# AdaLN block on one core: the feed-forward weight sums in two buffers, one sum emitted with each projection

## The chip, the cores and the metric

The kernel runs on one core of a Trainium2 chip. The metric is the device time of one execution in microseconds; the kernel before took 1318.79 us in the median of three runs (1311.11, 1318.79 and 1322.47). Engines are named as the profile names them: PE is TensorE (matmuls and transposes), DVE is VectorE, ACT is ScalarE, POOL is GpSimd, and SP is the sync engine, which here only issues DMAs. "SPq", "POOLq" and "ACTq" are the DMA-issuing instructions on those engines. Each engine runs its own instructions strictly in the order in which they were built, so an instruction that waits holds up all that stand behind it on its engine.

## The reference

The reference is one transformer block with adaptive layer norm, for 4 batches of 512 tokens of width 512, in float32:

```
mod = (silu(c) @ wmod)  ->  sa, ca, ga, sb, cb, gb          # per batch, width 512
h = layernorm(x) * (1 + ca) + sa
x = x + ga * attention(h)          # gated delta rule, 6 heads, key 64, value 128
h = layernorm(x) * (1 + cb) + sb
x = x + gb * ffn(h)                # (silu(h @ w_gate.T) * (h @ w_up.T)) @ w_down.T, hidden 2048
```

The attention projects h to q, k and v (each followed by a causal convolution of four taps and silu), to a gate, and to two small scalars per head and token (a decay and a beta). A recurrent state per head is decayed, corrected by the delta rule and read out token by token; the read-out is normalised, multiplied by silu(gate) and projected back to width 512. ga and gb are pushed away from zero to a size of at least 0.25.

## The kernel before, in words

Tokens are handled per batch b (0 to 3); a batch has four tiles of 128 tokens, and a tile two chunks of 64. The program has these parts:

- `first_normed_t`, `normed_t`: layer norm of a batch's x, and its transpose `ht` (features by tokens). `load_x(b)` brings the batch's x in, four chunks of 128 x 512. For batches 0 and 2 the four chunks are slices of one tile; for batches 1 and 3 they are four tiles of the tag `xt`, which has four buffers.
- `keys`, `queries`, `values`, `gates`: projections. One `weight` load (L249, on SP's queue, tag `w`, four buffers) serves one head or pair of heads, for the batches in its list. A projection is four matmuls (L478). Keys, queries and values go through `conv_silu` (ACT L486, three DVE operations L488, ACT L492). `by_token` turns a value projection to tokens (PE L559, DVE L561, tag `v`, two buffers) and stores it in DRAM from SP's queue (L565).
- `between(i)` is called after each projection of `values` and `gates`. It runs, on odd i, one step of the modulation for later batches.
- `triangles(b)`: the 32 x 32 triangular inverses of a batch. A chain of small DVE operations (L656, L660) ends in the tiles `ti` and `pm`, which SP stores to the DRAM tensors `td` and `ttd` (L664, L665); SP then loads them back in pieces (L709 to L711) as operands `t` and `lm`.
- `delta_rule(b)`: for each of four tiles, `operands` (PE L689 to L732), `scan` (PE L753, L762) and `finish` / `project` / `turned`. `finish` squares the output on POOL (L784, tile `osq`), and scales it on POOL (L790, tile `o`) once DVE has the norm; `project` transposes it (PE `pot` L799), multiplies by Wo (PE L803) and adds the residual on POOL (L806, tile `xr`); `turned` transposes the normed result `xn` (DVE L814, PE `pxn` L820). The PE work of other projections is interleaved with it.
- `weight_sums`: the feed-forward uses a seven-product scheme for 2 x 2 blocks of the gate and up weights, which needs four sums of weight blocks for each pair of hidden tiles. For each of 8 pairs and for the gate and the up weights (16 sums in all) it loads four blocks (four DMAs of 128 x 2 x 128 on SP's queue, L861), makes four additions on POOL (L866 to L869, each 128 x 256) and stores the 128 x 7 x 2 x 128 result to the DRAM tensor `wsum` from POOL's queue (L870). The tile is of the tag `wm`, which has one buffer, so the loads of one sum wait until the store of the sum before has landed. The tiles are called `wsg` (gate) and `wsu` (up) below.
- `feed_forward(b)` reads `wsum` back (L920, L921) and does the products (PE L927, L899).

The order of the work is the order of emission, reshaped by a scheduler: it places each engine's instructions by a priority (the place in the program) and by when it reckons that their inputs are ready. An instruction emitted early can so stand late on its engine, and an independent one emitted later can stand ahead of it. The emission around the change is: values, triangles and gates of batch 0, `delta_rule(0)`, keys and queries of batches 1 to 3, all of `weight_sums()`, then values and gates of batch 1, `triangles(1)`, values of batches 2 and 3, `delta_rule(1)`, gates of 2 and 3. On the engines, `delta_rule(0)` runs beside those keys, queries and sums.

Of the kernel before, what the change touches and what calls it, by code (L numbers as in the profile page):

```python
# [8 lines left out]
F32 = mybir.dt.float32  # L9
# [6 lines left out]
P = 128  # L16
B, T, D = 4, 512, 512
H, DK, DV = 6, 64, 128
FF = 2048
NT = T // P  # L20
# [17 lines left out]
def adaln_block(  # L38
# [29 lines left out]
    w1 = ctx.enter_context(tc.tile_pool(name="w1", bufs=1))  # L68
# [4 lines left out]
    pa_ = stage_a.enter_context(tc.tile_pool(name="pa", bufs=2))  # L73
# [77 lines left out]

    def load_x(b):

        if b in (0, 2):
            room = w1.tile([P, NT, D], F32, tag="hf", bufs=2, name=f"xt{b}")
        if b == 0:
            for c in (0, 2):
                sp.dma_start(
                    room[:, c : c + 2], x[b, c * P : (c + 2) * P, :].rearrange("(c p) f -> p c f", p=P)
                )  # L160
            return [room[:, c, :] for c in range(NT)]
        ts = []
        for c in range(NT):
            t = room[:, c, :] if b == 2 else pa_.tile([P, D], F32, tag="xt", bufs=4, name=f"xt{b}_{c}")
            if b < 3:
                after(t[:1, :1])
            (act if b > 2 else pool).dma_start(t, x[b, c * P : (c + 1) * P, :])
            ts.append(t)
        return ts
# [11 lines left out]
    early_load(act, 0)  # L181
    sp.dma_start(c_in, c_t.rearrange("(k p) b -> p k b", p=P))
    xts = load_x(0)
    early_load(sp, KD // 2)

# [1 line left out]
    act.activation(warm, eps, AF.Silu)  # L187
    act.activation(sc_t[:, :, :B], c_in, AF.Silu)

    last, steps = [], []  # L190

    def between(i):

        if i % 2 and steps:
            steps.pop(0)()


    def after(t):

        pool.tensor_copy(t, last[0][:1, :1])  # L200
# [68 lines left out]
    for i in range(2):  # L269
# [14 lines left out]
        t = stat.tile([P, H, C], F32, name=f"xs{i}")  # L284
# [224 lines left out]
    def keys(bs, hts):  # L509
        if bs == [0]:  # L510
            betas, store = decays(bs, hts)
        sk = {}
        for i, b in enumerate(bs):
            sk[b] = pa_.tile([P, H, NT], F32, tag=f"sk{i}", bufs=1, name=f"sk{b}")
        for p in range(NP):
            w = first_w if bs == [0] and p == 0 else weight(w_k, p, f"k{bs[0]}_{p}")
            for b in bs:
                n = f"k{b}_{p}"
                kt = conv_silu(w, cw["k"], p, hts[b], n)
                act.dma_start(kd[b][:, p, :], kt)  # L520
                lagging(lambda a=(kt, sk[b], p, 1.0, n): squares(*a), 3 if bs == [0] else 2)
            if p == 1 and bs != [0]:
                betas, store = decays(bs, hts)
            if p < 2 and bs == [0]:
                xts[p + 1] = load_x(p + 1)
            if p == (1 if bs == [0] else 2):
                store()
        def scalars():
            for i, b in enumerate(bs):
                act.activation(nk[b], sk[b], AF.Sqrt)  # L530
                pool.tensor_scalar(nk[b], nk[b], -1.0, None, ALU.mult)
                vec.reciprocal(sc[b], sk[b])
                vec.scalar_tensor_tensor(sc[b], sc[b], -1.0, betas[:, i], ALU.mult, ALU.mult)

        lagging(scalars)
# [12 lines left out]
    def values(bs, hts):  # L548
        for h in range(H):
            w = weight(w_v, h, f"v{bs[0]}_{h}")  # L550
            for b in bs:
                vt = conv_silu(w, cw["v"], h, hts[b], f"v{b}_{h}")
                lagging(lambda a=(b, h, vt): by_token(*a))
                between(h)
# [12 lines left out]
    def gates(bs, hts):  # L567
        for h in range(H):
            w = weight(w_g, h, f"g{bs[0]}_{h}")
            for b in bs:  # L570
                pg = projected(w, hts[b], f"g{b}_{h}")
                sg = pa_.tile([P, T], F32, tag="acc", bufs=4, name=f"sg{b}_{h}")
                act.activation(sg, pg, AF.Silu)
                act.dma_start(
                    sd[b][:, :, h, :].rearrange("c v i -> v c i"), sg.rearrange("p (c i) -> p c i", c=NT)
                )
                if tails:
                    tails.pop(0)()
                between(h)


    ex, at, td, ttd, hf = {}, {}, {}, {}, {}
# [255 lines left out]
    def complete():  # L838
        while pending:
            pending.pop(0)()  # L840
# [11 lines left out]
    def weight_sums():  # L852

        for i in range(NF // 2):
            for src, dst, nm in ((w_gate_t, wsum[0], "g"), (w_up_t, wsum[1], "u")):
                w = pa_.tile([P, 7, 2, P], F32, tag="wm", bufs=1, name=f"ws{nm}{i}")

                for a, rows in enumerate((w[:, 0:2], w[:, 4:7:2])):
                    cols = slice((2 * i + a) * P, (2 * i + a + 1) * P)
                    for h in range(2):  # L860
                        sp.dma_start(  # L861
                            rows[:, h],
                            src[h * TH : (h + 1) * TH, cols].rearrange("(k p) f -> p k f", p=P),
                        )
                a11, a12, s2, s1, a21, s4, a22 = (w[:, j] for j in range(7))
                pool.tensor_add(s1, a21, a22)  # L866
                pool.tensor_sub(s2, s1, a11)
                pool.tensor_sub(a21, a11, a21)
                pool.tensor_sub(s4, a12, s2)  # L869
                pool.dma_start(dst[i], w)  # L870
# [113 lines left out]
    for b in rest[2:]:  # L984
        hts[b] = normed_t(b, load_x(b))
# [4 lines left out]
    keys(rest, hts)  # L990
    queries(rest, hts)
    complete()
    weight_sums()
    values([1], hts)
    gates([1], hts)
    triangles(1)
# [65 lines left out]
```

## Time and profile before

| quantity | value |
|---|---|
| median of 3 runs (range) | 1318.79 us (1311.11 to 1322.47) |
| the profiled execution's own time | 1315.23 us |
| its span | 1313.5 us |
| PE busy | 1242.2 us, 95% |
| DVE busy | 713.9 us, 54% |
| ACT busy | 386.3 us, 29% |
| POOL busy | 249.3 us, 19% |
| mean granted PE clock | 0.98 |

Durations below come from the one profiled execution. Its time is 1.7 us more than its span, and 3.6 us less than the median. Idle time of an engine matters only where that engine holds up the end; PE is busy for 95% of the span, so about 71 us of it are left as PE idle time, plus what PE loses where its granted clock is below 1.

### The profile page before, as it was taken

Reading aid. Unit: us, or ns where it says so; the run is one execution under the profiler, and the core shown is the slowest. Engines: PE = TensorE matmul, PEld = TensorE weight load, DVE = VectorE, ACT = ScalarE, POOL = GpSimd, SP = SyncE. Lnnn points to the kernel's source line nnn. Section 1 sums busy time; section 2 is a strip of 40 time slices with the busy share of each in tenths; the row PEclk is TensorE's granted clock in tenths of the full one; section 3 lists DMA queues with packets and bytes.
Section 4 is the critical chain, followed back from the end, with each engine's and each line's share of the span. In section 5 each row is a group of like instructions: output and inputs, shape, how many; then the busy total and the mean of one; then the engine's idle time right before and its main releaser. Section 6 shows DMA issues by size and latency. Waiting matters only on the chain.

```text
span 1313.5 us, 18027 instructions
## 1 busy us (share of the span) xinstructions
PE 1242.2 (95%) x6620; PEld 777.2 (59%) x6620; DVE 713.9 (54%) x1547; ACT 386.3 (29%) x740; POOL 249.3 (19%) x299
## 2 busy tenths in 40 slices
PE   6899898899999998989999999899999999999998
PEld 3444355444444565757757666676666577576665
DVE  4767765555288245774445558644464444444443
ACT  3643346643142344211103332110234211011110
POOL 4210223543200012020021121011111201111111
PEclk9889999999999999999999999899999999999999
DMA  5979647767955447664335455443622243354331
GB/s 154 267 186 285 200 119 227 186 213 225 276 165 161 118 108 184 204 178 134 126 115 163 124 124 164 134 144 101 185 78 71 94 144 116 117 189 143 117 112 64
DMA packets 213271, 204.06 MB, mean 155 GB/s; under 512 B 95032, under 2 KB 163640, under 8 KB 213184
## 3 DMA queue, kind: packets, MB, share of 16 engines
q1 hardware_dynamic: 191408, 167.14, 44.6%
q0 software_dynamic: 4096, 20.99, 4.2%
q10 hardware_dynamic: 17680, 14.78, 3.5%
q8 instruction: 53, 0.87, 0.3%
q14 instruction: 34, 0.28, 0.1%
HBM read 152.94 MB, written 46.78 MB: 152 GB/s over the span
## 4 chain that ended last, share of the span: by engine, by line
PE 66%; DVE 13%; DMA 9%; POOL 4%; issue 3%; ACT 2%; SPq 1%; POOLq 0%; ACTq 0%; DVEq 0%
PE phg L927 15%; PE pd L899 15%; PE phu L927 11%; PE pwo L803 5%; PE pp_v L478 3%; PE pp_g L478 2%; PE pm L762 2%; DVE ti L660 2%; DVE tip L656 2%; PE scratch L689 2%; DMA wsum<-wsu 1%; PE pf L753 1%; DMA wsum<-wsg 1%; PE pp_k L478 1%; DMA wsg<-in_w_gate_t_dram 1%
## 5 line engine op out<-in xcount | busy, mean ns | idle before, releaser
L899 PE MATMUL pd<-wdn,hid 128*128 128x512 f32 x512 | 225.5, 593 | 0.0
L905 POOL TENSOR_TENSOR xm<-xm,tmpf 128x512 f32<-128x512 f32 x64 | 81.3, 1270 | 451.9 <-DVE tmpf L904 451.9
L899 PEld LDWEIGHTS pd<-wdn,hid 128*128 128x128 f32 x512 | 97.7, 191 | 109.2 <-issue 102.6
L927 PE MATMUL phg<-hf,wg 128*128 128x256 f32 x512 | 138.6, 388 | 0.3 <-DMA wg<-wsum 0.3
L927 PEld LDWEIGHTS phg<-hf,wg 128*128 128x128 f32 x512 | 96.4, 193 | 21.4 <-issue 7.3
L927 PE MATMUL phg<-hs,wg 128*128 128x256 f32 x384 | 103.4, 389 | 4.4 <-DVE hid L934 4.3
L927 PE MATMUL phu<-hf,wu 128*128 128x256 f32 x384 | 99.9, 384 | 2.1 <-DMA wu<-wsum 2.0
L904 DVE TENSOR_TENSOR tmpf<-pd,gb 128x512 f32<-128x512 f32 x64 | 44.1, 689 | 104.0 <-PE pd L899 93.0
L927 PE MATMUL phu<-hs,wu 128*128 128x256 f32 x384 | 96.1, 384 | 3.5 <-DVE up L940 3.5
L478 PE MATMUL pp_v<-ht,wv 128*128 128x512 f32 x192 | 93.6, 632 | 4.5 <-DVE v L561 2.3
L932 ACT COPY hid<-phg 128x256 f32<-128x256 f32 x32 | 11.9, 371 | 288.8 <-PE phg L927 286.5
L803 PE MATMUL pwo<-wo,ot 128*128 128x512 f32 x192 | 93.3, 617 | 0.0
L478 PE MATMUL pp_g<-ht,wg 128*128 128x512 f32 x192 | 91.4, 618 | 1.6 <-issue 1.6
L927 PEld LDWEIGHTS phu<-hs,wu 128*128 128x128 f32 x384 | 72.4, 191 | 22.0 <-DVE up L940 9.0
L927 PEld LDWEIGHTS phg<-hs,wg 128*128 128x128 f32 x384 | 71.6, 194 | 18.3 <-DVE hid L934 5.8
L927 PEld LDWEIGHTS phu<-hf,wu 128*128 128x128 f32 x384 | 71.3, 191 | 15.0 <-issue 5.2
L478 PEld LDWEIGHTS pp_v<-ht,wv 128*128 128x128 f32 x192 | 36.9, 202 | 46.2 <-issue 43.4
L488 DVE SCALAR_TENSOR_TENSOR acc_v<-pp_v,conv_v,acc_v 128x511 f32<-128x511 f32 (+2 forms) x72 | 53.3, 743 | 8.8 <-ACT acc_v L486 8.1
L478 PEld LDWEIGHTS pp_g<-ht,wg 128*128 128x128 f32 x192 | 35.1, 195 | 38.2 <-issue 37.0
L956 ACT ACTIVATE hid<-hid 128x1024 f32<-128x1024 f32 x32 | 33.8, 1057 | 79.9 <-DVE hid L940 63.5
L762 PE MATMUL pm<-r,l 128*128 128x128 f32 x384 | 52.7, 283 | 1.0 <-ACT r L758 0.8
L803 PEld LDWEIGHTS pwo<-wo,ot 128*128 128x128 f32 x192 | 34.4, 192 | 30.1 <-issue 28.3
(236 smaller groups left out, 1812.8 us busy)
## 6 DMA issues: line engine op xcount, KB each, us to landing
wdn<-in_w_down_t_dram SPq DMA_DIRECT2D x32, 512.0 KB, 4.3
wg<-wsum SPq DMA_DIRECT2D x32, 512.0 KB, 3.7
wu<-wsum SPq DMA_DIRECT2D x32, 512.0 KB, 3.6
wg<-wsum SPq DMA_DIRECT2D x32, 384.0 KB, 4.3
wu<-wsum SPq DMA_DIRECT2D x32, 384.0 KB, 4.4
wsum<-wsg POOLq DMA_DIRECT2D x8, 896.0 KB, 4.0
wsum<-wsu POOLq DMA_DIRECT2D x8, 896.0 KB, 4.5
wg<-in_w_g_dram SPq DMA_DIRECT2D x24, 256.0 KB, 3.2
```

The lines of the kernel that those rows point to most:

```text
L478: pe.matmul(pp, w[:, k, :], ht[:, k, :], start=(k == 0), stop=(k == KD - 1))
L488: vec.scalar_tensor_tensor(acc[:, i:], pp[:, : T - i], taps[:, col, TAPS - 1 - i : TAPS - i], acc[:, i:], ALU.mult, ALU.add,)
L656: vec.tensor_tensor(v, pm[:, j, j + 1 :, None].broadcast_to([n, m, j]), t[:, j : j + 1, :j].broadcast_to([n, m, j]), ALU.mult,)
L660: vec.tensor_add(t[:, j + 1 :, :j], t[:, j + 1 :, :j], v)
L689: pe.matmul(pv[:, u, 2 * par : 2 * par + 2, :], kc[i][us, p, par : par + 2, :], qc[i][us, p, par : par + 2, :], start=True, stop=True,)
L762: pe.matmul(pm[:, h], l[:, hs.start + h, 2 * par : 2 * par + 2, :], r[:, par, hs.start + h], start=True, stop=True,)
L803: pe.matmul(pw, ot[:, h, :], wo[:, h, :], start=(h == 0), stop=(h == H - 1))
L899: pe.matmul(pd, hids[q, i // 2][:, i % 2, c * P : (c + 1) * P], wdn[q, i // 2][:, i % 2, :], start=(i == 0), stop=(i == NQ - 1),)
L904: vec.tensor_mul(tmp, pd, gb)
L905: pool.tensor_add(xm[c], xm[c], tmp)
L927: pe.matmul(o, l[:, k], r[:, k], start=k == 0, stop=k == 1)
L956: act.activation(hid, hid, AF.Silu)
```

## The change

All 16 sums stay, with the same loads, additions and stores. Three things move:

- `weight_sums` becomes a generator that stops ahead of each sum. `between` advances it by one step after each projection of `values` and `gates`. The first step only reaches the first stop, so the 16 sums are emitted after the 2nd to the 17th of those projections: five with the values of batch 1, six with its gates, five with the values of batches 2 and 3.
- The gate sums keep the buffer of tag `wm`; the up sums take the buffer of tag `xt`. Both tiles are declared as 128 x 4 x 512 and the first 14 x 128 columns are used.
- The x of batches 1 and 3 is one tile of tag `xt` with one buffer, instead of four tiles with four buffers. The bytes are the same.

```diff
     def load_x(b):
-        if b in (0, 2):
-            room = w1.tile([P, NT, D], F32, tag="hf", bufs=2, name=f"xt{b}")
+        room = (w1 if b in (0, 2) else pa_).tile(
+            [P, NT, D], F32, tag="xt" if b % 2 else "hf", bufs=1 if b % 2 else 2, name=f"xt{b}"
+        )
...
         for c in range(NT):
-            t = room[:, c, :] if b == 2 else pa_.tile([P, D], F32, tag="xt", bufs=4, name=f"xt{b}_{c}")
+            t = room[:, c, :]
...
-    last, steps = [], []
+    last, steps, sums = [], [], []
     def between(i):
         if i % 2 and steps:
             steps.pop(0)()
+        if sums and next(sums[0], 1):
+            sums.clear()
...
         for i in range(NF // 2):
             for src, dst, nm in ((w_gate_t, wsum[0], "g"), (w_up_t, wsum[1], "u")):
-                w = pa_.tile([P, 7, 2, P], F32, tag="wm", bufs=1, name=f"ws{nm}{i}")
+                yield
+                room = pa_.tile([P, NT, D], F32, tag="wm" if nm == "g" else "xt", bufs=1, name=f"ws{nm}{i}")
+                w = room.rearrange("p c f -> p (c f)")[:, : 14 * P].rearrange(
+                    "p (j k f) -> p j k f", j=7, k=2
+                )
...
     complete()
-    weight_sums()
+    sums.append(weight_sums())
     values([1], hts)
```

## The prediction

> **What bounds the kernel now.** I read the page's busy shares first: PE is busy for 95% of the span, so a change pays only where it closes a PE gap or lifts PE's granted clock. Then the chain that ended last, cut to the stretch in which the sums run (120 to 365 us):
>
> ```profile
> 311.75 2.67 DMA wsg<-in_w_gate_t_dram
> 314.59 0.71 POOL wsg L866
> ...
> 317.78 3.88 DMA wsum<-wsg
> 322.13 0.46 SPq L861
> ...
> 346.86 0.51 SPq L861
> 347.46 3.84 DMA wv<-in_w_v_dram
> 351.44 1.10 PE pp_v L478 x2
> ```
>
> From 257 us on this chain holds no PE work at all: load, four additions, store, next load, sixteen times one after the other in one buffer, until a value weight (wv) that stood behind the last sum on SP's queue comes in and PE goes on. What SP waits for, in the waits of its queue (us in all, times, longest):
>
> ```profile
> SPq L861 <- DMA wsum<-wsg: 31.7, 7, 7.2
> SPq L861 <- DMA wsum<-wsu: 30.0, 5, 7.6
> ```
>
> So SP stands 61.7 us in front of a sum's load, waiting for the store ahead to land, and whatever is behind on the queue is late by that. What this costs PE, in the waits of PE from 150 to 160, 210 to 260 and 320 to 356 us:
>
> ```profile
> PE scratch L717 <- DMA t<-td: 3.5, 1, 3.5
> ...
> PE pxn L820 <- DVE xn L814: 3.3, 2, 2.3
> PE pot L799 <- POOL o L790: 1.9, 1, 1.9
> PE pot L799 <- POOL gyt L460: 1.5, 1, 1.5
> ...
> PE pvt L559 <- DVE v L561: 3.1, 1, 3.1
> PE pp_v L478 <- DMA wv<-in_w_v_dram: 1.8, 1, 1.8
> PE pp_g L478 <- issue: 1.6, 1, 1.6
> ```
>
> A gap costs more than its length. In the table by stretch (length; busy and count of PE, PEld, DVE, ACT, POOL; clock; DMA share; GB/s) the clock is 1.00 before the gap at 154 to 158 us, and then:
>
> ```profile
> 155.00:160.00 5.00, 2.16 (x20) 0.93 (x20) 1.21 (x3) 0.51 (x1) 0.00 (x0) 0.85 0.59 163
> 160.00:165.00 5.00, 5.00 (x33) 1.91 (x32) 1.12 (x2) 1.77 (x4) 0.00 (x0) 0.50 0.25 39
> 165.00:170.00 5.00, 5.00 (x51) 1.89 (x50) 0.36 (x1) 0.62 (x2) 0.00 (x0) 0.96 0.22 66
> ```
>
> That is 5 x (0.15 + 0.50 + 0.04) = 3.45 us of PE's work lost. The same sum gives 1.6 us after the gaps at 215 to 225 (clock 0.68 in 225 to 230) and 0.4 + 1.3 = 1.7 us around the gap at 327 (0.92, then 0.74).
>
> The Trainium skill ("TensorE: Matmul & The Clock Gate", "What's actually happening") says that PE's clock halves after an idle window of about 3.4 us. The drop after 225 us follows gaps of 1.1, 1.2 and 1.5 us only; by the rule, a middle stage like it would not drop, and the sum below would end 1.6 us less far down at its best end.
>
> **The change, part by part.** Nothing is added on any engine: 64 loads, 64 additions (0.73 us) and 16 stores before and after. Only waits and places change. I compared the order in which the two kernels, as built, stand on each engine.
>
> *A. td behind a sum (154 to 166 us).* DVE ends the chain of batch 0's triangles at 147.3 us (last L660), but SP issues the store td only at 152.22, because the first load of the third sum stands ahead of it and waits for the second sum's store until 151.8. In the changed order the first up sum has its own buffer: its loads stand at about 129 to 135 us instead of 139.3 to 141.4, its additions follow the gate's (131.5 to 134.7), so they run at about 137.5 to 140.4, and with 4.3 us of store it lands near 145. The load that stands ahead of td waits for this store. td so goes out when DVE is done, at 147.5 to 149: 3.2 to 4.7 us earlier, against a PE wait of 3.5. With the gap, the half clock behind it goes. Ends: nothing (if the additional 2.8 MB of a second pair of sums, some 11 us at the 250 GB/s of this stretch, push the store's landing back to 151) and 3.5 + 3.45 = 6.9 us. I take 6, near the upper end, since td has 3 us to spare over what is needed.
>
> *B. The end of delta_rule(0) (215 to 256 us).* PE is busy for 32.7 of these 41 us; with the clock the stage can give 8.3 + 1.6 = 9.9 us, and the other end is a loss: POOL now has 11 sums instead of 6 ahead of the second tile's scaling, on which PE's pot waits:
>
> ```profile
> 222.23 0.73 POOL L869 TENSOR_TENSOR wsu<-wsu 128x256 f32<-128x256 f32 x1
> 223.26 0.60 POOL L870 DMA_DIRECT2D wsum<-wsu  x1 [0.30 <-POOL wsu L869]
> 223.88 1.48 POOL L790 TENSOR_TENSOR o<-o,ms 128x768 f32<-128x768 f32 x1
> ```
>
> DVE's part of it is ready at 220.9, so POOL's sum costs 3 us here. I followed the new queue on from A: the fifth gate sum and the first half of the fifth up sum stand ahead of the first xr; they are loaded at about 195.5 and 200 and added until 205.4, 2 us late for a scan that is 6 us ahead. xn, xr of the second tile and the last of the sixth gate sum's loads follow it (about 213), the additions run until 219, and the scaling starts at 219, 4.9 us earlier than now. So about 1 to 2 us of A are given back here. Then the order helps: xr of the second tile (now 237.35, held 2.2 us by a sum; tmpa was ready at 235.2) and the scaling of the third tile have no late sum ahead, and the DVE scans of batch 1 (1.2 and 3.93 us, now between 239 and 246) stand earlier: the waits of 2.3 and 1.9 us go. Together +2 us, nearer to nothing than to 9.9, because the first half shifts waits rather than ends them.
>
> *C. The gates and values after it (323 to 353 us).* Three stalls are SP's lateness: v (its buffer is freed by a store that stood behind a sum), a gate weight (shown as "issue"; its load went out at 325.4) and wv. In the new order all 64 loads stand ahead of the second value weight of batch 1, so none is left in front of these. 3.1 + 1.6 + 1.8 + 1.7 of clock = 8.2 us at most; nothing at the other end, if the sums come out as late as now. I take 7. PE was busy without a gap from 256 to 323 us, so it is PE itself that comes earlier. What is late next is DVE in 353 to 430 us (18 of each 20 us); it starts earlier by as much, since it idles from 323 to 353 (4.8 us busy in 30).
>
> *D. Crowding.* 16 instead of 12 sums stand ahead of the last xmid store of delta_rule(0): four more times four issues of 0.47 us, and 5.6 MB, some 25 us at 225 GB/s in a stage whose DMA share is 0.56 to 0.69. Hidden behind PE's filled 166 to 215 and 256 to 323 us; if not, each issue is late by up to 2 us per sum. I take -1; ends 0 and -8 (four sums by 2 us).
>
> The Trainium skill ("SBUF — State Buffer", "Who interferes with whom") speaks against crowding: a DVE operation in a two-port mode is blocked for the whole of a GpSimd instruction. Here xn took 1.67 us beside osq at 215.2 and 0.55 otherwise; by the rule a sum's addition beside each of four xn would make D up to 2.9 us worse.
>
> *E. x as one tile.* The instructions and the waits of each chunk are the same in both orders; nothing, either way up to 0.5 us for one issue.
>
> Sum: 6 + 2 + 7 - 1 = 14 us, from the profiled execution's 1315.2: **1301 us**. The median of the runs shown is 3.6 us above that execution, so 1301 is 1.3% below the median; runs of this kernel lie 11 us apart, and about 1% (13 us) is what a measurement can tell from no change.
>
> **The rivals.**
>
> 1. *The middle gives A back.* If the second tile's scaling on POOL comes no earlier than 224 us, A's 6 are gone at 224 and only C stays: 1315 - 7 = 1308. For it: 11 sums are ahead of it and each needs a landing; against it, the 4.9 us worked out above.
> 2. *The change doesn't act.* The sums still come one after the other, since SP issues in order and each load waits for scan operands ahead of it: stalls move but stay, 0 to 3 us, 1313. Against: the buffer that a load waits for was freed one sum earlier.
> 3. *Slower: the scan of batch 0 becomes bound by the sums.* Place: POOL, the scaling of the second tile behind the 11th sum. The first sum is added at 131.5; the 11th holds the scaling up beyond today's 223.9 once a sum takes more than (223.9 - 131.5) / 10 = 9.2 us. Where nothing else stood ahead, one buffer took 12.0 us a sum (first additions at 290.2 to 349.9, five intervals), so two buffers should take 6 to 7. If the two do not overlap and it stays at 11, the scaling comes at about 245: 21 us late, 1.7 more of clock, less C's 7: 1331.
>
> **How the numbers follow.** Forecast (A and C open, B about even) 0.55, around 1301 (1291 to 1306); rival 1 0.25, 1306 to 1311; rival 2 0.10, 1311 to 1316; rival 3 0.10, beyond 1316. Best end 1315.2 - 6.9 - 9.9 - 8.2 = 1290. The range from 1291 to 1314 leaves out rival 3 and part of rival 2. Faster by over 1% (under 1305.6): most of the forecast, 0.49; within 1%: 0.43; slower by over 1% (above 1332): the worse part of rival 3, 0.08.
>
> **What the changed profile would show.** A: td issued before 149 us, no wait of L717 at 154, and no half clock at 160. B: the second L790 between 217 and 221. C: the last sum's store before 300 us, and no wait of pvt, pp_g or pp_v between 320 and 356. The forecast is wrong if td is still late, if L790 is at 224 or later, or if the gaps come back further down, above all in 353 to 430 us.

## The result, and the profile after

The changed kernel took 1324.59 us in the median of 20 runs, beside 1318.04 us for the kernel before in runs of the same sessions: a ratio of **1.0057 (95% interval 1.0038 to 1.0076)**, some 7.5 us slower by that ratio (the two medians are 6.6 apart). One run of each kernel was far slower than all the others (1429.61 us before, 2077.62 after) and is left out of the ratio. The forecast was 1301, with a range that ended at 1314, so the kernel became slower where I had expected it to become faster. The profiled execution of the changed kernel took 1328.37 us (span 1326.7). Lines of the changed kernel stand 3 further down than before (L793 is the scaling that was L790, L809 the residual addition), and those of the sums 7 (L868 loads, L873 to L876 additions, L877 store).

What SP stands in front of, by its waits between 120 and 360 us (us in all, times, longest), is what the change set out to shorten, and it did shorten it:

```profile
SPq L868 <- DMA wsum<-wsg: 11.6, 2, 7.2
...
SPq L868 <- DMA wsum<-wsu: 5.1, 2, 4.5
```

That is 16.7 us in place of 61.7. PE's waits in the same stretch tell the other half:

```profile
PE pot L802 <- POOL o L793: 6.2, 1, 6.2
PE scratch L692 <- DVE yk L703: 4.8, 1, 4.8
PE scratch L720 <- DMA t<-td: 3.9, 1, 3.9
```

The wait for `t`, which part A was to remove, is there with 3.9 us (3.5 before). The wait for `o`, 1.9 us at the third tile before (`pot` at 250.78), is now 6.2 us at the fourth (`pot` at 288.12). The one for `yk` has grown from 0.4 to 4.8, and the waits for v, wv and the gate weight between 320 and 356 us are gone. The table by stretch (length; busy and count of PE, PEld, DVE, ACT, POOL; clock; DMA share; GB/s) shows the same by stage, before:

```profile
215.00:256.00 41.00, 32.70 (x251) 19.74 (x250) 25.07 (x47) 27.87 (x55) 22.80 (x28) 0.96 0.66 179
256.00:323.00 67.00, 67.00 (x355) 33.59 (x354) 37.02 (x64) 31.85 (x54) 22.46 (x30) 1.00 0.69 216
323.00:353.00 30.00, 23.62 (x118) 10.65 (x116) 4.83 (x7) 4.10 (x7) 9.56 (x14) 0.94 0.88 268
```

and after:

```profile
215.00:256.00 41.00, 32.86 (x294) 22.45 (x295) 21.24 (x44) 26.94 (x53) 25.72 (x37) 0.88 0.81 241
256.00:323.00 67.00, 60.05 (x316) 30.79 (x315) 33.31 (x62) 34.69 (x57) 21.90 (x28) 0.92 0.55 169
323.00:353.00 30.00, 30.00 (x121) 14.66 (x120) 15.73 (x23) 10.80 (x19) 0.00 (x0) 1.00 0.48 140
```

So the stretch from 256 to 323 us, which had no gap, now has gaps of 7 us in all and a lower clock (0.92 in place of 1.00), and the last one is filled.

Before, the chain of waits that ended last held no PE work from 257 us on. Now it holds none between 213 and 238 us, where it runs through two sums and two operations of the scan on POOL:

```profile
213.84 1.30 SPq L868
...
216.23 3.94 DMA wsu<-in_w_up_t_dram
...
221.10 0.72 POOL wsu L874
221.83 1.22 POOL xr L809
...
224.71 5.43 DMA wsum<-wsu
...
233.51 0.71 POOL wsg L874
...
236.51 1.48 POOL o L793
```

The reader sees `xr` (the residual addition of the first tile) after two additions of an up sum, and `o` (the scaling of the second tile) after those of a gate sum. PE's `pot` follows `o` at 238.04; it had waited 1.3 us there (1.5 before).

Where the time went is read from the same instructions in both kernels. The times are starts in us from the start of each span; the changed kernel was profiled twice (1328.37 and 1322.69 us), since its first profile had lost 2 us already at 129 us, ahead of all that the change touches.

| first start of | before | after | after, second profile |
|---|---|---|---|
| a key projection ahead of the sums (the 25th pp_k) | 128.9 | 131.0 | 128.9 |
| store td | 152.2 | 154.8 | 152.7 |
| PE pm, the scan's first | 175.7 | 181.7 | 178.2 |
| the first xr | 209.5 | 221.8 | 218.1 |
| the second o | 223.9 | 236.5 | 232.8 |
| the third o | 249.3 | 258.3 | 256.3 |
| the fourth o | 269.9 | 286.6 | 283.6 |
| values of batch 1 (the 49th pp_v) | 296.0 | 316.4 | 311.8 |
| values of batch 2 (the 97th pp_v) | 351.4 | 363.4 | 358.8 |
| the first feed-forward product (phg) | 518.1 | 533.6 | 527.5 |

In the second profile the kernel is level with before until td, 2.5 us late at pm, 8.6 late at the first xr, 13.7 at the fourth o, 15.8 at the values of batch 1; then it wins 8.4 back by 351 us (the first profile: from 20.4 to 12.0, 8.4 as well), is 7.4 us late there and 9.4 at the feed-forward.

The lower clock is part of this. Between 120 and 460 us the granted clock was a half for 20.5 us before and for 47.8 and 44.4 us after. PE was busy for 19.9 us of that before and for 43.7 and 40.5 after; one us of work at half clock would take half a us at full clock, so that is some 10 to 12 us. These stretches follow the gaps: one starts at 287.2 us, within the wait for `o` that ended at 288.1, and lasts 10.2 us. The total of one profile varies, though: x_before_dve below, as fast as the kernel before, had 34.1 us of half clock between 120 and 460 us. Between 120 and 330 us alone it is 11.0 us before, 7.0 in x_before_dve and 34.1 in both profiles of the changed kernel.

### The profile page after: what moved, and what is told of

Same layout as the page of the kernel before. It is cut to its first block, busy times and chain, and to the rows that moved or that the text cites. A ratio compares the mean times of both kernels' runs of the same rounds, so it can differ in the third digit from the quotient of the medians.

```text
span 1326.7 us, 18019 instructions
## 1 busy us (share of the span) xinstructions
PE 1254.0 (95%) x6620; PEld 784.3 (59%) x6620; DVE 713.8 (54%) x1547; ACT 392.0 (30%) x744; POOL 250.2 (19%) x299
## 4 chain that ended last, share of the span: by engine, by line
PE 74%; DVE 12%; DMA 6%; POOL 3%; issue 2%; ACT 2%; SPq 1%; POOLq 0%; ACTq 0%; DVEq 0%
PE phg L934 15%; PE pd L906 14%; PE phu L934 11%; PE pwo L806 7%; PE pp_v L481 6%; PE pp_g L481 4%; PE pp_q L481 3%; PE pm L765 2%; DVE ti L663 2%; DVE tip L659 2%; PE pp_k L481 2%; PE scratch L692 2%; PE pf L756 1%; PE scratch L735 1%; PE scratch L720 1%
## 5 line engine op out<-in xcount | busy, mean ns | idle before, releaser
L934 PEld LDWEIGHTS phu<-hf,wu 128*128 128x128 f32 x384 | 71.4, 191 | 14.5 <-issue 4.6
L481 PE MATMUL pp_q<-ht,wq 128*128 128x512 f32 x96 | 50.7, 669 | 2.4 <-DVE acc_k L491 2.4
```

Source lines behind the costliest of these rows:

```text
L481: pe.matmul(pp, w[:, k, :], ht[:, k, :], start=(k == 0), stop=(k == KD - 1))
L934: pe.matmul(o, l[:, k], r[:, k], start=k == 0, stop=k == 1)
```

## The experiments

All ratios are to the kernel before, run on the same chip in the same session, with 95% intervals.

| run | what it is | ratio |
|---|---|---|
| x_two_buffers | two buffers, sums emitted together as before | 1.0034 [1.0007, 1.0060] |
| x_emit_only | one buffer, one sum with each projection | 1.0030 [1.0005, 1.0055] |
| x_one_tile | before, x of batches 1 and 3 as one tile | 0.9974 [0.9952, 0.9995] |
| x_scan_on_dve | after, scan of batch 0 without POOL | **0.9962 [0.9942, 0.9983]** |
| x_before_dve | before, scan of batch 0 without POOL | 1.0012 [0.9983, 1.0040] |
| x_sums_tied | after, each sum's loads held until its projection | 1.0132 [1.0105, 1.0160] |
| x_tied_pool_queue | the same, those loads on POOL's queue | 1.0241 [1.0202, 1.0279] |
| x_after_pool_queue | after, the sums' loads on POOL's queue | 1.0088 [1.0055, 1.0121] |
| x_before_td_act | before, td and ttd of batch 0 on ACT's queue | 1.0082 [1.0054, 1.0111] |
| x_after_td_act | after, the same | 1.0126 [1.0097, 1.0155] |
| x_one_pair | before, 2 of the 16 sums | 0.9862 [0.9815, 0.9908] |
| x_after_again | after, one run | no ratio |

### The three parts of the change, each alone

The second buffer without the new place of emission (from the changed kernel):

```diff
-                yield
                 room = pa_.tile([P, NT, D], F32, tag="wm" if nm == "g" else "xt", bufs=1, name=f"ws{nm}{i}")
...
-    sums.append(weight_sums())
+    weight_sums()
```

> The changed kernel with the sums emitted where they were before (all 16 ahead of the values of batch 1), the two buffers and x as one tile kept. If the two buffers are the cause (sums that start earlier stand ahead of the scan of batch 0 on POOL and SP and crowd its transfers), it is 4 to 10 us slower than the kernel before, like the changed kernel. If the place of the emission is the cause, it is within 2 us of the kernel before or faster.

The new place of emission without the second buffer (from the kernel before, with the lines of `between` that the change adds):

```diff
+                yield
                 w = pa_.tile([P, 7, 2, P], F32, tag="wm", bufs=1, name=f"ws{nm}{i}")
...
-    weight_sums()
+    sums.append(weight_sums())
```

> The kernel before with the sums emitted one with each projection, but still in one buffer, x as before. If the buffers are the cause: within 3 us of the kernel before, since one buffer paces the sums as before and POOL's order is the same. If the emission is the cause: 4 to 10 us slower.

And x as one tile alone, in the kernel before:

```diff
-            room = w1.tile([P, NT, D], F32, tag="hf", bufs=2, name=f"xt{b}")
+        room = (w1 if b in (0, 2) else pa_).tile(
+            [P, NT, D], F32, tag="xt" if b % 2 else "hf", bufs=1 if b % 2 else 2, name=f"xt{b}"
+        )
```

> The kernel before with only x of batches 1 and 3 as one tile. All theories of the sums: within 2 us of the kernel before. If it is 3 us or more slower, the tile of x has a part in the loss.

The second buffer (with x as one tile, which it needs) gives 1.0034, and it alone shows the loss in the middle: the first xr at 220.9, the second o at 235.7, the fourth at 285.0, and 47.8 us of half clock between 120 and 460 us. The first xr stands 6.9 us behind a sum on POOL there, as in the changed kernel (6.9); the later lateness sits elsewhere, since its third o comes at 266.5 (258.3 in the changed kernel). The emission alone leaves POOL's order as it was, and the second o (225.1) and the fourth (272.1) stay within 2.2 us of before; it still measured 1.0030, with an interval that nearly reaches 1, and no cause for it was found. One tile for x has the same order of instructions on all five engines as before and measured 0.9974, again with an interval that ends close to 1. So by these profiles, one of each kernel, the loss in the middle comes with the second buffer. The ratios alone don't divide the 1.0057 between buffer and emission.

### The scan of batch 0 without POOL

If the sums on POOL's queue hold up the scan, then taking the scan's three POOL operations (squares, scaling, residual) to DVE for batch 0 must remove the loss and leave part C's gain. In the changed kernel, and as a control in the kernel before:

```diff
-        pool.tensor_mul(osq, o, o)
+        eng = vec if b == 0 else pool
+        eng.tensor_mul(osq, o, o)
...
-        pool.tensor_tensor(o, o, ms[:, :, None].broadcast_to([P, H, DV]), ALU.mult)
+        eng.tensor_tensor(o, o, ms[:, :, None].broadcast_to([P, H, DV]), ALU.mult)
...
-        pool.tensor_add(xr, xr, tmp)
+        (vec if b == 0 else pool).tensor_add(xr, xr, tmp)
```

> The changed kernel with the squaring, the scaling and the residual addition of batch 0's delta rule on VectorE instead of GpSimd. Theory queue (the sums ahead on GpSimd hold these three): the stage of 215 to 323 us loses its waits for o and xr, and the kernel is 6 to 14 us faster than the changed one, so 7 us faster to 1 us slower than the kernel before. Theory crowding (late landings hold the scan whatever engine runs it): it stays 4 to 9 us slower than the kernel before.

> Control: the kernel before with the same three operations of batch 0's scan on VectorE. Its waits for o and xr in 215 to 256 us are 3.4 us, and one half clock of 1.7 us hangs on them: 0 to 5 us faster. If it gains as much as the changed kernel does by the same edit, the sums on GpSimd are not what the edit shows.

The changed kernel becomes 0.9962, 12 to 13 us faster than with the scan on POOL (1.0057) and some 5 us faster than the kernel before; the kernel before gains nothing by the same edit (1.0012). Of the 5 us, some 3 may belong to x as one tile (0.9974), which this kernel has too. PE's waits in x_scan_on_dve, 120 to 360 us:

```profile
PE scratch L720 <- DMA t<-td: 8.4, 1, 8.4
PE pot L803 <- ACT o L773: 2.9, 1, 2.9
```

No wait of PE names POOL any more, and the one for `yk` is 0.3 us. The second o comes at 223.9, the fourth at 274.0, and values of batch 2 at 349.2, 2.2 us ahead of before, although PE now stands 8.4 us in front of `t`. So the hold on POOL's queue is what the change made worse. Part C's gain is real too: PE comes to the values of batch 1 at 295.2, no later than before (296.0), and from there to the values of batch 2 it is idle for 1.2 us in place of 6.4, so these waits are gone because the sums are done, not because PE comes later. The 8.4 us are also of use below: there td goes out at 150.96, and the first load of `t` only at 158.37.

### The sums held back until their projections

> The changed kernel with each sum's loads held until the convolution of the projection with which it is emitted has written its first element (a copy of one element into the sum's tile), so that no sum stands beside the scan of batch 0. Both theories: the scan of batch 0 runs without waits for sums, the third-tile scaling of GpSimd comes before 245 us, no half clock between 220 and 300. What it costs is new: the sums' loads stand among the weight loads of batch 1's values and gates (PE is full there), about 6 us a sum in two buffers, 16 sums in 100 us. 4 to 12 us faster than the kernel before if these loads stay hidden, up to 8 slower if they hold the weights back.

Two one-element copies on POOL tie a sum's loads to the projection that it was emitted with:

```diff
+                after(w[:1, 0, 0, :1])
+                after(w[:1, 4, 0, :1])
                 for a, rows in enumerate((w[:, 0:2], w[:, 4:7:2])):
```

The additions of all 16 sums now stand between 301 and 423 us. The kernel is 17 us slower than before, outside what was expected (12 faster to 8 slower). Without the sums the front runs as parts A and B had hoped and better: td at 146.6, pm at 167.4 (8.3 us earlier than before), the second o at 205.2 and the fourth at 251.7. All of it is lost again further down, in the values that the sums stand beside; PE's waits between 120 and 460 us:

```profile
PE pp_v L481 <- DVE v L564: 15.5, 3, 11.4
PE pp_v L481 <- DMA wv<-in_w_v_dram: 5.1, 1, 5.1
```

and SP's from 290 to 460 us, where it stands in front of the sums' loads again, with the value weights and the stores of v behind it:

```profile
SPq L870 <- DMA wsum<-wsg: 39.6, 7, 8.0
```

If SP's queue were all of it, the loads could be issued by POOL, which has to wait for the same stores anyway:

```diff
-                        sp.dma_start(
+                        pool.dma_start(
```

> As the run with the sums held behind the projections, but with the sums' loads issued by GpSimd instead of SP, so that nothing of SP's queue stands behind them. In that run the scan of batch 0 came 20 us earlier than in the kernel before (third scaling at 229 against 249 us) and all of it was lost after 300 us, where SP stood in front of the sums' loads (15.5 us of waits for v, 5.1 for a value weight). Theory queue (the sums cost by what stands behind them on an in-order queue): the waits for v and for the value weight go, the scan keeps its lead, 5 to 20 us faster than the kernel before. Theory crowding (their transfers cost wherever they run): the weights and stores of batch 1 land late all the same, within 3 us of the kernel before or slower.

> The changed kernel with only the sums' loads moved to GpSimd's queue. Theory queue: SP's part of the loss goes (the loads ahead of td, of the first xmid, of the last xr), GpSimd's part stays or grows by four more issues of about 0.7 us a sum ahead of the scan's three operations: between 4 us faster and 10 us slower than the kernel before. Theory crowding: as the changed kernel, 5 to 9 us slower than the kernel before, with td still at 152 to 156 us.

Both became slower, by 32 and 12 us: the first where the theory of the queue had 5 to 20 us faster, the second a little beyond the ranges of both theories. In x_tied_pool_queue the ties themselves took SP's place: ACT may not write the next `acc_v` before POOL has read the old one, and POOL reads it late. ACT's waits between 300 and 460 us, and behind them PE's:

```profile
ACT acc_v L489 <- POOL wsg L203: 36.6, 2, 33.7
```

```profile
PE pvt L562 <- ACT acc_v L495: 32.8, 3, 21.5
```

In x_after_pool_queue the loads stand on the very queue that the scan waits for: the first xr comes at 225.3 and the second o at 242.2, later than with SP (221.8 and 236.5).

### td away from SP's queue

To see whether the place of td behind a sum's load is what part A depends on, batch 0's two stores were put on ACT's queue, in the kernel before and in the changed one:

```diff
-        sp.dma_start(td[b], t)
-        sp.dma_start(ttd[b], pm)
+        (sp if b else act).dma_start(td[b], t)
+        (sp if b else act).dma_start(ttd[b], pm)
```

> The kernel before with the two stores of batch 0's triangular inverses (td, ttd) issued by ScalarE instead of SP, so that no sum's load stands ahead of them. If part A of the prediction was priced rightly (3.5 us of wait and 3.45 us of half clock hang on that store), it is 4 to 7 us faster than the kernel before; if something else holds PE there (another load behind the sums, or the products of the scan), within 2 us.

> The changed kernel with the same two stores issued by ScalarE. If the td store behind the fourth sum's loads is a part of the loss: 3 to 7 us faster than the changed kernel. If the loss is all in the scan behind the sums on GpSimd: within 2 us of the changed kernel, 5 to 9 us slower than the kernel before.

Both missed what was expected: 11 us slower than before (expected: 4 to 7 faster, or within 2 us), and 9 us slower than the changed kernel (expected: 3 to 7 faster, or within 2 us). td went out earlier (149.9 and 151.7 us), and PE waited longer for `t`: 9.2 and 15.4 us. SP's timeline in x_after_td_act says why:

```profile
150.83 1.91 SPq L868 DMA_DIRECT2D wsu<-in_w_up_t_dram  x4
161.14 0.88 SPq L868 DMA_DIRECT2D wsg<-in_w_gate_t_dram  x2
162.12 2.46 SPq L712 DMA_DIRECT2D t<-td  x3
```

The loads of `t` are still SP's, and the scheduler now put the next gate sum's loads ahead of them, waiting until 161.14 for the gate store before. In x_before_td_act it is the same with the sum at 157.91 and `t` at 159.91. The hold moved from the store of td to the load behind it; the edit does not tell what part A is worth without any hold.

### All but one pair of sums left out

```diff
-        for i in range(NF // 2):
+        for i in range(1):
...
-            sp.dma_start(w[:, :4], src[i // 2][:, :4])
-            sp.dma_start(w[:, 4:], src[i // 2][:, 4:])
+            sp.dma_start(w[:, :4], src[0][:, :4])
+            sp.dma_start(w[:, 4:], src[0][:, 4:])
```

> The kernel before with only the first pair of sums made, which the feed-forward reads eight times, so 14 of the 16 sums are left out. It gives the price of the sums where they stood. By the prediction's ceilings (6.9 for td, 9.9 for the end of the scan, 8.2 for the stretch after it) it is at most 25 us faster than the kernel before; 10 to 25 if the sums cost what the waits showed, under 8 if PE's gaps there have other causes that only stood behind the sums.

This kernel leaves out 14 of the 16 sums and reads the first pair in place of the others; it bounds roughly what any arrangement of the sums can win. It is 18 us faster than before (0.9862 x 1318.0 = 1299.8). The forecast of 1301 had thus asked of the change nearly all that the sums cost. Its scan runs some 14 us earlier from the second tile on, so the stage of part B stands at 200 to 242 us in it:

```profile
200.00:242.00 42.00, 40.49 (x360) 25.87 (x356) 22.89 (x53) 32.20 (x62) 11.10 (x18) 1.00 0.38 93
```

PE is busy for 40.49 of 42 us at a clock of 1.00, against 32.70 of 41 at 0.96 before. So the gaps of this stage are nearly all the sums' doing: 1.5 us of 8.3 stay without them. Most of the 9.9 us that were part B's upper end are there to be had, but this change didn't get them.

> The changed kernel once more, for a second profile. What belongs to the order of the queues comes back within 1 us: the waits of PE for o (6.2 us), for yk (4.8) and for td (3.9), and the first residual addition 11 us after the kernel before's. What belongs to the phase of the clock's windows may differ by 20 us of half clock between 120 and 460 us.

The second profile is the last column of the first table. It is level with before until td and shows the same waits with 5.3 us (`o`), 4.4 (`t`) and 4.3 (`yk`), within 1 us as expected; the first xr is 8.6 us after the one before, not 11.

## Why the prediction was wrong

**A, td behind a sum: predicted +6, measured -2.5 by pm in the second profile.** The step that failed is "its additions run at about 137.5 to 140.4, and with 4.3 us of store it lands near 145". The changed kernel on POOL, in order of time (start, length, what it waited for in brackets):

```profile
134.21 0.72 POOL L873 TENSOR_TENSOR wsg<-wsg 128x256 f32<-128x256 f32 x1 [12.76 <-DMA wsg<-in_w_gate_t_dram]
...
137.72 0.61 POOL L877 DMA_DIRECT2D wsum<-wsg  x1 [0.30 <-POOL wsg L876]
143.60 0.71 POOL L873 TENSOR_TENSOR wsu<-wsu 128x256 f32<-128x256 f32 x1 [5.27 <-DMA wsu<-in_w_up_t_dram]
...
146.92 0.57 POOL L877 DMA_DIRECT2D wsum<-wsu  x1 [0.30 <-POOL wsu L876]
152.68 1.47 POOL L873 TENSOR_TENSOR wsg<-wsg 128x256 f32<-128x256 f32 x1 [5.19 <-DMA wsg<-in_w_gate_t_dram]
```

and on SP:

```profile
145.16 1.97 SPq L868 DMA_DIRECT2D wsg<-in_w_gate_t_dram  x4
...
153.30 1.44 SPq L868 DMA_DIRECT2D wsu<-in_w_up_t_dram  x3
154.84 0.41 SPq L667 DMA_DIRECT2D td<-ti  x1
...
158.45 3.13 SPq L712 DMA_DIRECT2D t<-td  x3
```

The up sum's additions start 6 us later than reckoned (2 to 3 of them this profile's own late start), because its loads, with the gate sum's store and the next sums' loads beside them, land late; its own store, issued at 146.92, lets SP go on at 153.30, after 6.4 us instead of 4.3. The second profile shows it without the late start. There the additions start at 140.88, 3.4 us later than reckoned, the store again takes 6.4 us until SP goes on, and td follows behind three of the next sum's loads:

```profile
144.22 0.57 POOL L877 DMA_DIRECT2D wsum<-wsu  x1 [0.30 <-POOL wsu L876]
```

```profile
150.59 2.06 SPq L868 DMA_DIRECT2D wsu<-in_w_up_t_dram  x3
152.75 0.41 SPq L667 DMA_DIRECT2D td<-ti  x1
```

The chain of triangles had ended at 148.0, so td stood 4.7 us behind a sum, as against 5.0 before (147.25 to 152.22): the hold that part A was to end was still there. I had named this end ("if the additional 2.8 MB of a second pair of sums [...] push the store's landing back to 151") and had given it too little weight.

In the DMA view from 120 to 170 us the medians to landing rose from 3.8 to 4.4 us (loads of wsg), 3.3 to 5.5 (loads of wsu), 4.2 to 7.2 (stores of wsg) and 4.2 to 5.3 (stores of wsu), and the mean rate from 200 to 260 GB/s; the second profile has 3.5, 5.3, 6.3 and 5.2 at 245 GB/s. The chain of triangles itself ended at 152.5 in the first profile (147.3 before), with half clock from 143.8, and at 152.8 in x_after_pool_queue, where no sum's load stands on SP and td waited for the chain alone. That this stage can give as much as I hoped is shown by x_sums_tied, where no sum is near: td goes out when the chain ends and pm comes 8.3 us earlier, more than the 6.9 of my upper end. One profile of each kernel is little to read 2.5 us from, but they agree: from the key projection of the table to pm it is 45.8 to 47.4 us in before, x_before_dve and x_emit_only, and 49.3 to 52.4 in the two profiles of the changed kernel, x_two_buffers and x_scan_on_dve. How A's failure divides between the wait on SP's queue, slow landings and the chain stays open. A landing can do it: in x_scan_on_dve td went out 1.3 us earlier than before, but took 7.4 us from its issue to the first load of `t` (3.0 in x_one_pair and x_sums_tied, 3.6 in before and the first profile), and PE waited 8.4 us. The queue can do it as well, as x_after_td_act shows.

**B, the end of delta_rule(0): predicted +2, measured -13.3, with what follows it (from 2.5 us late at pm to 15.8 at the values of batch 1, in the second profile).** Of this, 4.5 us are lost by the third o, about where the stage of part B ends, and 8.8 after it, in the stretch that terms C and D took as filled by PE's other work. The sign was wrong, and the step is "they are loaded at about 195.5 and 200 and added until 205.4", of the sums ahead of the first xr, which goes with "two buffers should take 6 to 7" us a sum. The gate sum was loaded at 210.07 and the up sum at 213.84, and they were added until 221.8. The changed kernel on POOL:

```profile
197.71 1.47 POOL L793 TENSOR_TENSOR o<-o,ms 128x768 f32<-128x768 f32 x1 [3.67 <-DVE ms L792]
199.14 0.72 POOL L873 TENSOR_TENSOR wsg<-wsg 128x256 f32<-128x256 f32 x1
...
202.34 0.60 POOL L877 DMA_DIRECT2D wsum<-wsg  x1 [0.30 <-POOL wsg L876]
...
216.27 0.72 POOL L873 TENSOR_TENSOR wsg<-wsg 128x256 f32<-128x256 f32 x1 [8.98 <-DMA wsg<-in_w_gate_t_dram]
...
221.78 1.26 POOL L809 TENSOR_TENSOR xr<-xr,tmpa 128x512 f32<-128x512 f32 x1
...
232.70 0.72 POOL L873 TENSOR_TENSOR wsg<-wsg 128x256 f32<-128x256 f32 x1 [4.45 <-DMA wsg<-in_w_gate_t_dram]
...
236.51 1.48 POOL L793 TENSOR_TENSOR o<-o,ms 128x768 f32<-128x768 f32 x1
```

The operand of that first `xr`, `tmpa`, was ready 6.9 us before it:

```profile
214.23 0.69 DVE L808 TENSOR_TENSOR tmpa<-pwo,ga 128x512 f32<-128x512 f32 x1 [1.48 <-PE pwo L806]
```

In the kernel before, `xr` followed its `tmpa` (ready at 209.25) almost at once:

```profile
209.50 1.28 POOL L806 TENSOR_TENSOR xr<-xr,tmpa 128x512 f32<-128x512 f32 x1
```

So the first xr lost 6.6 us on POOL to the fifth gate sum and half of an up sum (6.7 us of hold in the second profile, 6.9 in x_two_buffers, 0.4 in x_emit_only and x_scan_on_dve).

Why the sums were not faster shows in their rounds. The first sum's additions start at 134.21 and the 11th's at 232.70: 9.85 us a sum. Over all 16, the stores go from 138 to 294 us, 10.4 us a sum (14.5 before, from 135 to 353). Where the forecast rested on a round of 12.0 us for one buffer, and so 6 us a sum with two, the first round of the gate buffer took 18.5 us (134.21 to 152.68; 15.1 in the second profile). Nothing of the scan stands on POOL in it, and SP waits only for the store: 3.5 us from the first addition to the store, 7.4 until SP goes on with the next loads (145.16), 7.5 until these are in. With two sums under way, the landing of the store and the loads took this long by themselves. Later rounds also wait for SP: the third gate sum's loads go out at 175.35, 18.7 us after the store ahead of them (156.62), behind the scan's loads of `t` and `lm`, and the fourth's at 194.35 behind more of the scan's loads. Over its seven rounds the gate buffer took 21.7 us a round. So the two buffers overlap, but a round is longer in both of its parts, landings and places on the queue, and the sums and the scan hold each other up: the sums' loads wait behind the scan's on SP, and the scan's operations behind the sums' on POOL. How the loss divides between the two parts no run shows.

**Rival 3 was right in its mechanism and wrong in its place.** It had the scan held by sums on POOL and the period from which that decides (9.2 us a sum; it was 9.85). The place that it named, the scaling of the second tile behind the 11th sum, came 12.6 us late (8.9 in the second profile), but was held no longer than before: its norm was ready at 233.6 and it ran at 236.51, 2.9 us later, as against 3.0 before. It was late because the first xr had been. Its price, 1331, went by a period of 11. The hold grew at two other places, the first xr (0.3 to 6.9 us) and the fourth o (2.3 to 6.8; 6.0 in the second profile). As the prediction had it, the holds of the second xr (2.2) and PE's wait at the third o (1.9) went: the lateness fell from 8.9 to 7.0 us there in the second profile.

From the first xr the hold reaches PE through DVE, where the statistics of `xr` stand ahead of `yk`, on which PE waits (4.8 us):

```profile
223.08 0.69 DVE L296 BATCH_NORM_STATS2 st<-xr 128x6 f32<-128x512 f32 x1 [5.88 <-POOL xr L809]
...
226.22 0.41 DVE L703 TENSOR_TENSOR yk<-scratch,y 128x256 f32<-128x256 f32 x1
```

And the fourth o stands behind the last gate sum, on SP

```profile
273.78 3.28 SPq L868 DMA_DIRECT2D wsg<-in_w_gate_t_dram  x2
280.50 0.34 SPq L785 DMA_DIRECT2D xr<-in_x_dram  x1
280.88 0.95 SPq L868 DMA_DIRECT2D wsg<-in_w_gate_t_dram  x2
```

where two of that sum's loads stand behind a load of x, which waits for the third tile's store of xmid, and on POOL

```profile
285.91 0.72 POOL L873 TENSOR_TENSOR wsg<-wsg 128x256 f32<-128x256 f32 x1 [10.45 <-DMA wsg<-in_w_gate_t_dram]
286.60 1.47 POOL L793 TENSOR_TENSOR o<-o,ms 128x768 f32<-128x768 f32 x1
```

so that the scan's fourth tile waits, through a sum, for the store of its third. I had taken 256 to 323 us as filled by PE's other work, since it had been so before; that cover went when PE's independent projections were used up in the earlier gaps (this last link is argued from the order of the work, not shown by a run).

**C, the gates and values behind it: predicted +7, measured +8.4**, in both profiles (up to 0.9 of it, and as much of the loss ahead, is 20 small matmuls that now stand ahead of the first of these values). The last sum's store is at 294 us (predicted: before 300), PE is busy for 30.00 of 30 us from 323 to 353, and none of the waits for v, wv and the gate weight is left. **D, crowding: predicted -1**, as late issues. It came as late landings instead, inside A and B, as the first round of the gate buffer shows, and no run separates its price; `xn` took 1.80 us beside `osq` at 226.7 us, as it had taken 1.67 before. **E, one tile:** predicted nothing, either way up to 0.5 us; measured 0.9974, some 3 us, with an interval that ends 0.6 us from no change.

The sum by the second profile's own numbers is -2.5 (A) - 13.3 (B and what follows) + 8.4 (C) = -7.4 us at 351 us, and the ratio of the runs gives 7.5 us; that they agree so closely is in part luck, since single profiles of one kernel differ by several us. The forecast had 1301 = 1315 - 6 - 2 - 7 + 1: C was right, and A and B were wrong by 8.5 and 15 us.

## What to carry to other kernels

A second buffer shortens only the wait for the buffer: before counting on a shorter period, follow one whole round through every in-order queue on which its steps stand, with landings as long as they are when two are under way (here a round grew from 12.0 us to between 15.1 and 18.5 with nothing else between its steps, and to 21.7 with the scan's loads among them), and count that each piece of background work that is pulled ahead is one more that the critical work can stand behind. Moving the few critical operations to an engine without the background work was worth more here (12 to 13 us against the changed kernel, some 5 against the one before) than any arrangement of the background that was run, and a bound from a run that leaves the work out (18 us here) tells when a forecast asks too much.

## What the runs showed of the hardware that was not expected

- Landings were longer where more was under way: with 260 in place of 200 GB/s in 120 to 170 us (a DMA share of 0.84 in place of 0.68 to 166 us), the median of loads of 128 KB went from 3.3 and 3.8 us to 5.5 and 4.4 (wsu and wsg), that of stores of 896 KB from 4.2 to 5.3 and 7.2; each is a median of two to eight DMAs, or a single one for the stores before. With a queue that waits for a landing, this is latency on the path.
- The half clock follows gaps far shorter than its own length: in the changed kernel 6.8 us of it start at 143.8, with gaps of 1.60 us (ending at 143.2) and 1.37 us (ending at 145.2) around it. The Trainium skill ("TensorE: Matmul & The Clock Gate", "What's actually happening") speaks of an idle window of some 3.4 us; the stretches here do come as 3.4, 6.8, 10.2, 13.7 and 17.1 us, multiples of such a window, but the gaps ahead need not fill one.
- A kernel with the same order of instructions on all five engines (x_one_tile) measured 0.26% below before. Differences of some 3 us can so stand in a ratio of many runs without any cause that the order shows, and the ratios of 1.0030 and 1.0034 above carry no more than that each by itself.
